# Turning all softmax tiles in place on VectorE, with stepped keys and four-term weights

## The chip, the cores and the metric

The kernel runs on one core of a Trainium2 chip, as a single launch. The metric is device time in microseconds (us); the time of a version is the median of its runs. A profiled execution gives the span from the first to the last instruction, which is a little shorter than the device time of the same execution.

## What is computed

A transformer block in float32 for 4 sequences (batches) of 512 tokens of width 512: a layer norm, and on its result both an attention with 16 heads and an MLP, added to the input. The MLP's weights are not stored but interpolated from control points by a cubic spline.

```python
xn = layernorm(x)                                     # x: (4, 512, 512)
q, k, v = (xn @ W + b for each of q, k, v)            # 16 heads of 32
scores = q k^T / sqrt(32) + slope[h] * arange(-511, 1)   # by key
attn = softmax(where(causal, scores, lowest))
ctx = attn v
a = ctx @ Wo + bo
gate_w, up_w = spline(gate_cp), spline(up_cp)         # (2048, 512)
down_w = spline(down_cp)                              # (512, 2048)
m = (silu(xn @ gate_w^T) * (xn @ up_w^T)) @ down_w^T
out = x + a + m
```

`spline` evaluates a Catmull-Rom cubic: every weight is a sum of four neighbouring control points times four coefficients that depend only on the weight's place.

## The kernel before

The kernel has two phases. The attention phase (to about 388 us of the span) holds the norms, the projections, the softmax and the making of most of the interpolated weights; the MLP phase follows, batch after batch.

**Units and groups.** Heads are taken four at a time: a group is one batch and four heads (`hg`), and there are 16 groups, g = 0 to 15, four to a batch. A unit is one group and one block `i` of 128 queries, so a group has four units; unit `i` has `i+1` blocks of 128 keys below the diagonal. A loop over `n`, one step per unit and three more at the end (`LAG`), writes out the order by hand; the helper `in_order` then keeps each engine's instructions in the order in which they were issued. In step `n`:

- `scores` multiplies queries by keys on TensorE into four PSUM banks, one per head (L865; a single set of banks, which the next unit reuses), and VectorE adds the distances and takes the extreme in one pass into the tile `p{i}` (L878), one buffer per `i`;
- `exponentials` runs on ScalarE (ACT; L894), in place;
- `normalize` takes the reciprocal of the sums on VectorE (L907) and multiplies on GpSimd (POOL; L909), for the unit of the step before;
- turning, so that keys lie across partitions for the product with the values. Two ways are mixed. Key blocks 0 and 2 are turned by TensorE, 128x128 at a time against the identity, into PSUM (L922, `turn`, three steps late), and copied by ACT to `pT` (L923). Key blocks 1 and 3 (`SLOTS`) are turned by VectorE in blocks of 32x32 into a tile of their own, `blocks` (L937, `swap`, two steps late), and four transfers on the SP queue, one for each strip of 32 partitions, put the blocks in place in `moved` (L945), which has one buffer;
- `values` (L966), once a group: 16 matmuls from `pT`, `moved` and `v` into one bank, called c here; ACT copies it out (L981). For group g they are issued in the last step of group g+1.

Since the two ways leave the keys of a block in different orders, ACT writes kT in halves (L816, L817), the second half stepped by four, and there are two distance tables, `dists`.

Around this, `items` and `small` put work into chosen steps: the projections of q and k for the next group (L798), of v (L837), the turning of the normed input (L767 on VectorE, L782, L783), the output projection of the batch before (L482, L489), the moments of the input that the MLP needs (`stretch_moments`, L510 to L525), input loads. POOL issues copies of laid-out rows to DRAM (L546). With a budget of microseconds a step, `some_weights` puts in VectorE's multiply and add steps of the weights: the row weights (gate and up, 8 terms, L646 and L649, coefficients times points that are broadcast to 32 partitions), and after them the down weights (5 and 4 terms, L690 and L693).

**The MLP phase** follows the strings in `plans`: G is a gate product of a quarter of the hidden width, U an up product (with its product on VectorE, L1157, a copy on POOL, L1158, and transfers), V an up product in the other set of banks, P an output projection of the last batch, F a load of features, X copies of rows, m, M, R, S, T moments and sums for the down product, L a load of the residual.

Of the kernel before, what the change touches and what calls it, by code (L numbers as in the profile page):

```python
# [18 lines left out]
P = 128  # L19
# [4 lines left out]
NB = D // P  # L24
# [6 lines left out]
SLOTS = [(1, 1), (2, 1), (3, 1), (3, 3)]  # L31
# [17 lines left out]
NCV = 5  # L49
NX = 9 + 4  # L50

COPIES = (1, 1, 4, 1)
NW, NW4 = 11, 4
NST = NW4 + 1

DOWN_STEPS = [("v", lo, hi, c) for lo, hi in ((0, 5), (5, 9)) for c in range(NCV)]
DOWN_STEPS += [("m", 0, NB, c) for c in range(4)]
# [277 lines left out]

def own_points(parts, points):


    values = parts[:, :, :, :9].transpose(0, 4, 3, 1, 2)
    values = values.reshape(P, 9, 2, P // 2, NCD)  # L340
    moments = parts[:, :, :, 9:].transpose(3, 4, 0, 1, 2)
    moments = moments.reshape(P, NB, 2, P // 2, NCD)
    strip = np.broadcast_to(points[:, None, None], (NB, Q32, 9, P, NCD)).reshape(values.shape)
    group = np.broadcast_to(points[None], (P, NB, P, NCD)).reshape(moments.shape)
    own = {}
    for kind, a, number, n in (("v", values, strip, NCV), ("m", moments, group, 4)):
        hit = (a != 0.0).any(axis=3)
        first = np.where(hit.any(axis=3), hit.argmax(axis=3), 0)
        first = np.minimum(first, NCD - n)[:, :, :, None, None] + np.arange(n)
        first = np.broadcast_to(first, (*a.shape[:4], n))  # L350
        few = np.take_along_axis(a, first, axis=4)
        assert np.count_nonzero(few) == np.count_nonzero(a)
        shape = (*a.shape[:2], P, n)
        own[kind] = few.reshape(shape), np.take_along_axis(number, first, axis=4).reshape(shape)
    steps = [[a[:, lo:hi, :, c].reshape(-1) for a in own[k]] for k, lo, hi, c in DOWN_STEPS]
    return *(np.concatenate(a) for a in zip(*steps)),
# [20 lines left out]
_coef = _coef.reshape(NB, NB, P, NCG, 2, Q32).transpose(3, 1, 5, 0, 4, 2)  # L377
COEF = single(_coef.reshape(NCG, P, NB, 2, P))
# [20 lines left out]
def block_kernel(  # L399
# [67 lines left out]
    dists = [wp.tile([P, S], F32, name=f"dist{k}") for k in range(2)]  # L467
# [35 lines left out]
    def stretch_moments(b):  # L503
# [15 lines left out]
        for k, ps in enumerate(banks):  # L519
            n = 64 if k == 2 else P  # L520
            o = xtp.tile([P, S], F32, name="out", bufs=2)
            if k == 1:
                nc.scalar.copy(o[:n], ps[:n])
            else:
                nc.vector.tensor_copy(o[:n], ps[:n])  # L525
            for s, (at, half) in place.items():
                if at == k:
                    nc.sync.dma_start(out=rows[s], in_=o[half * 64 : (half + 1) * 64])
# [23 lines left out]
    with ExitStack() as att:  # L552
# [36 lines left out]
        for k, dist in enumerate(dists):  # L589
            for t in range(NB):  # L590
                part = dist[:, t * P : (t + 1) * P]
                shape, steps = part, [[1, P]]
                if t % 2 == k:
                    shape = part.rearrange("p (r y) -> p r y", y=Q32)
                    steps = [[1, NB], [NB, Q32]]
                nc.gpsimd.iota(
                    shape,
                    pattern=steps,
                    base=1 - S + t * P,
                    channel_multiplier=0,  # L600
                    allow_small_or_imprecise_dtypes=True,
                )
                if t == NB - 1:
                    nc.gpsimd.affine_select(
                        out=shape,
                        in_=shape,
                        pattern=[[-step, n] for step, n in steps],
                        compare_op=ALU.is_ge,
                        fill=NEG,
                        base=0,  # L610
                        channel_multiplier=1,
                    )
# [3 lines left out]
        def row_weight_steps(first_down):  # L616
            size = NB * 2 * P
            shaped = lambda a: a.rearrange("p (q x n) -> p q x n", q=NB, x=2)
            spare = [
                feat[0].rearrange("p c h s -> p (c h s)")[:, k * size : (k + 1) * size]  # L620
                for k in range(4)
            ]
            temps = [wd[:, :size], wd[:, size : 2 * size]]
            tabs, points = {}, {}

            def load(c):
                def go():
                    tabs[c], points[c] = (shaped(a) for a in spare[c % 2 * 2 :][:2])
                    nc.sync.dma_start(out=tabs[c], in_=coef[c])
                    for k in range(NB):  # L630
                        strip = slice(k * Q32, (k + 1) * Q32)
                        nc.sync.dma_start(
                            out=spare[c % 2 * 2 + 1][strip],
                            in_=rowpts[c, k].partition_broadcast(Q32),
                        )
# [3 lines left out]
            def term(c, w):  # L639
                to = wT[:, :, 2 * w : 2 * w + 2, :]  # L640
                tmp = shaped(temps[w]) if c else to

                def times():
                    own = points[c].rearrange("p (w q) x n -> p w (q x) n", w=2)[:, w]
                    own = own.unsqueeze(2).to_broadcast([P, NB, 2, P])
                    nc.vector.tensor_tensor(tmp, tabs[c], own, ALU.mult)  # L646

                def plus():
                    nc.vector.tensor_tensor(to, to, tmp, ALU.add)  # L649

                return [times, plus] if c else [times]

            steps = [(0.0, load(0)), (0.0, load(1))]
            for c in range(NCG):
                for w in range(2):
                    steps += [(1.2, half) for half in term(c, w)]
                if c + 2 < NCG:
                    steps.append((0.0, load(c + 2)))
                elif c + 2 == NCG:
                    steps += first_down  # L660
            return steps


        def down_steps():
            size = 5 * P
            spare = feat[0].rearrange("p c h s -> p (c h s)")
            given, at = [], 0
            for _, lo, hi, _ in DOWN_STEPS:
                given.append((at, (hi - lo) * P))
                at += P * (hi - lo) * P  # L670

            def load(n):
                def go():
                    at, width = given[n]
                    for k, source in enumerate((downtab, downpts)):
                        to = spare[:, (n % 3 * 2 + k) * size :][:, :width]
                        part = source[at : at + P * width].rearrange("(p x) -> p x", p=P)
                        nc.sync.dma_start(out=to, in_=part)

                return go  # L680

            def term(n):
                kind, lo, hi, c = DOWN_STEPS[n]
# [679 lines left out]
```

## Time and profile before

| | |
|---|---|
| device time, median of 3 runs | 544.58 us (543.7 to 544.58) |
| device time of the profiled execution | 543.63 us |
| its span | 541.4 us |
| granted TensorE clock, mean | 0.993 |
| bytes moved by transfers | 92.98 MB |

The profile names a group of instructions by the line of the program, the engine, the operation and the tiles, output first (`p<-s,dist`). PE is TensorE's matmuls, PEld its loading of weights, DVE VectorE, ACT ScalarE, POOL GpSimd, SP the engine that issues most transfers; a trailing q is an engine's queue. Behind the bar of a group stand its busy time, the mean of one instruction, and the idle time just before the group with what ended it. A float32 matmul is recorded twice, a transpose once. The ends of matmuls are modelled, and neighbours on one engine overlap by some tenths of a microsecond, so a row's sum can be above what the engine was held.

### The profile page before, as it was taken

Reading aid. Unit: us, or ns where it says so; the run is one execution under the profiler, and the core shown is the slowest. Engines: PE = TensorE matmul, PEld = TensorE weight load, DVE = VectorE, ACT = ScalarE, POOL = GpSimd, SP = SyncE. Lnnn points to the kernel's source line nnn. Section 1 sums busy time; section 2 is a strip of 40 time slices with the busy share of each in tenths; the row PEclk is TensorE's granted clock in tenths of the full one; section 3 lists DMA queues with packets and bytes.
Section 4 is the critical chain, followed back from the end, with each engine's and each line's share of the span. In section 5 each row is a group of like instructions: output and inputs, shape, how many; then the busy total and the mean of one; then the engine's idle time right before and its main releaser. Section 6 shows DMA issues by size and latency. Waiting matters only on the chain.

```text
span 541.4 us, 12182 instructions
## 1 busy us (share of the span) xinstructions
PE 530.3 (98%) x4268; PEld 268.0 (50%) x4268; DVE 352.8 (65%) x990; ACT 296.0 (55%) x798; POOL 243.8 (45%) x436
## 2 busy tenths in 40 slices
PE   7999999999999999999999999989999999999997
PEld 6645545444445544444554454545334555747552
DVE  6169978888677877667676456563135584865836
ACT  2466875665466665646757588883313433624222
POOL 3045635574266565446656567671017232332310
PEclk9999999999999999999999999979999999999999
DMA  8933487575545785745743325464656565665344
GB/s 317 321 122 70 114 213 215 160 194 155 161 144 147 243 276 166 214 142 146 215 123 89 92 67 148 137 188 118 174 165 197 184 221 197 199 203 181 119 164 166
DMA packets 63805, 92.98 MB, mean 172 GB/s; under 512 B 10528, under 2 KB 35104, under 8 KB 63232
## 3 DMA queue, kind: packets, MB, share of 16 engines
q1 hardware_dynamic: 59136, 83.79, 51.5%
q0 software_dynamic: 4608, 8.40, 5.3%
q8 instruction: 34, 0.56, 0.4%
q14 instruction: 27, 0.22, 0.1%
HBM read 50.74 MB, written 23.68 MB: 137 GB/s over the span
## 4 chain that ended last, share of the span: by engine, by line
PE 84%; DVE 5%; DMA 5%; ACT 3%; SPq 2%; issue 1%; DVEq 0%; ACTq 0%
PE mm L798 17%; PE g L1135 9%; PE mm L837 9%; PE s L865 7%; PE mm L922 7%; PE mm L482 6%; PE o L1236 6%; PE c L966 5%; PE o L1182 4%; PE o L1253 3%; PE o L482 3%; ACT p L894 2%; DVE p L878 2%; PE s L482 2%; PE mm L510 2%; PE o L1135 2%
## 5 line engine op out<-in xcount | busy, mean ns | idle before, releaser
L909 POOL TENSOR_SCALAR p<-p,inv 128x128 f32<-128x128 f32 (+3 forms) x256 | 147.5, 589 | 172.1 <-DVE inv L907 122.1
L894 ACT ACTIVATE p<-p,low 128x128 f32<-128x128 f32 (+3 forms) x256 | 141.3, 555 | 48.9 <-DVE low L878 48.3
L878 DVE CUSTOM_DVE_ANT_0 p<-s,dist 128x128 f32<-128x128 f32 (+3 forms) x256 | 108.8, 481 | 21.8 <-PE s L865 21.5
L1158 POOL COPY made<-inner 128x512 f32<-128x512 f32 x64 | 38.9, 637 | 104.2 <-DVE inner L1157 81.5
L923 ACT COPY pT<-mm 128x512 f32<-128x512 f32 x96 | 54.8, 577 | 40.3 <-PE mm L922 40.0
L1135 PE MATMUL g<-feat,wT 32*64 32x512 f32 x864 | 65.3, 592 | 0.0
L1150 ACT ACTIVATE act<-g 128x512 f32<-128x512 f32 x64 | 33.0, 602 | 57.0 <-PE g L1135 56.7
L865 PE MATMUL s<-kT,qT 32*128 32x512 f32 (+3 forms) x512 | 57.4, 479 | 2.2 <-DVE low L878 2.0
L798 PE MATMUL mm<-xnT,wk 128*128 128x512 f32 (+1 forms) x136 | 59.3, 579 | 0.2 <-ACT xnT L783 0.2
L837 PE MATMUL mm<-wv,xnT 128*128 128x512 f32 x128 | 58.1, 596 | 1.1 <-ACT xnT L783 1.1
L798 PE MATMUL mm<-xnT,wq 128*128 128x512 f32 (+1 forms) x136 | 57.8, 567 | 0.0
L922 PE MATMUL mm<-ident,p 128*128 128x128 f32 x384 | 56.5, 283 | 0.4 <-ACT pT L923 0.3
L922 PEld LDWEIGHTS mm<-ident,p 128*128 128x128 f32 x384 | 42.5, 142 | 25.6 <-issue 17.1
L894 ACT ACTIVATION_READ_ACCUMULATOR p<-p,low 128x1 f32 x256 | 48.8, 191 | 0.0
L937 DVE STREAM_TRANSPOSE blocks<-p 128x512 f32<-128x512 f32 x64 | 43.4, 696 | 0.0
L1157 DVE TENSOR_TENSOR inner<-g,act 128x512 f32<-128x512 f32 x44 | 27.3, 683 | 21.7 <-PE g L1135 10.7
L1135 PEld LDWEIGHTS g<-feat,wT 32*64 32x64 f32 x864 | 30.6, 131 | 21.3 <-issue 10.6
L865 PEld LDWEIGHTS s<-kT,qT 32*128 32x128 f32 x512 | 24.5, 186 | 32.8 <-issue 16.2
L798 PEld LDWEIGHTS mm<-xnT,wk 128*128 128x128 f32 x136 | 24.5, 189 | 25.1 <-issue 21.5
L546 POOL DMA_DIRECT2D table<-samples x64 | 36.9, 583 | 0.0
L1236 PE MATMUL o<-inner,dRM 32*64 32x512 f32 x512 | 36.6, 588 | 0.0
L798 PEld LDWEIGHTS mm<-xnT,wq 128*128 128x128 f32 x136 | 24.7, 190 | 22.4 <-issue 21.7
(105 smaller groups left out, 656.3 us busy)
## 6 DMA issues: line engine op xcount, KB each, us to landing
moved<-blocks SPq DMA_DIRECT2D x128, 64.0 KB, 2.1
moved<-blocks SPq DMA_DIRECT2D x64, 128.0 KB, 3.0
feat<-table SPq DMA_DIRECT2D x16, 512.0 KB, 4.3
inner<-made SPq DMA_DIRECT2D x32, 256.0 KB, 3.5
table<-samples POOLq DMA_DIRECT2D x64, 88.0 KB, 3.0
xp<-in_xp_dram SPq DMA_DIRECT2D x16, 256.0 KB, 5.1
feat<-in_coef_dram SPq DMA_DIRECT2D x8, 512.0 KB, 8.8
feat<-in_rowpts_dram SPq DMA_DIRECT2D x32, 128.0 KB, 5.1
```

The source lines that it names most:

```text
L482: nc.tensor.matmul(ps, lhsT=wsb["o"][:, c, r * P : (r + 1) * P], rhs=ctxT[b][:, c, :], start=(c == 0), stop=(c == NB - 1),)
L798: nc.tensor.matmul(ps[0][:, tokens], lhsT=wsb[name][:, c, hg * P : (hg + 1) * P], rhs=xnT[b][:, c, tokens], start=(c == 0), stop=(c == NB ...
L837: nc.tensor.matmul(ps[0], lhsT=xnT[b][:, c, t * P : (t + 1) * P], rhs=wsb["v"][:, c, :], start=(c == 0), stop=(c == NB - 1),)
L865: nc.tensor.matmul(banks[b, hg][j][:, at : at + (k + 1) * P], lhsT=qk[b, hg, "q"][rows, k * P : (k + 1) * P], rhs=qk[b, hg, "k"][rows, : ( ...
L878: nc.vector.tensor_tensor_reduce(out=p[:, j, :nk], in0=ps[j], in1=dists[i % 2][:, S - nk :], scale=-SLOPES[hg * NG + j], scalar=BIG, op0=A ...
L894: nc.scalar.activation(p[:, j, :nk], p[:, j, :nk], AF.Exp, bias=low[:, j : j + 1], scale=-1.0, accum_out=total[:, j : j + 1],)
L909: nc.gpsimd.tensor_scalar(p[:, j, :nk], p[:, j, :nk], inv[:, j : j + 1], 1.0, ALU.mult, ALU.mult)
L922: nc.tensor.transpose(ps[:, j, :], p[:, j, c * P : (c + 1) * P], ident)
L923: nc.scalar.copy(pT[b, hg, c][:, :, (i - c) * P : (i - c + 1) * P], ps)
L937: nc.vector.transpose(own[:, :, k].rearrange("p r j k -> p j r k"), soft[u][0][:, :, c * P : (c + 1) * P].rearrange("p j (r k) -> p j r k" ...
L1135: nc.tensor.matmul(ps[k][cols, :], lhsT=wT[rows, q, 2 * w + part, cols], rhs=feat[b][rows, q, part, :], start=(part == 0), stop=(part == 1),)
L1236: nc.tensor.matmul(sums[b][r][cols, :], lhsT=dR[rows, a, cols], rhs=o[rows, :], start=(a == 0), stop=False,)
```

## The change

- **Turning.** `turn`, `pT` and their ACT copies are gone. `p` is laid out as (strip r, key block c, head, 32), `swap` turns the whole tile in place with one VectorE instruction per unit (512, 1024, 1536 or 2048 elements a partition), and four transfers per unit move it to `moved`, now with 13 slots, one buffer. Row block 0's move is held until after the value matmuls of the group before have been issued.
- **Keys.** All keys of a block are in one stepped order: ACT writes kT with one instruction, TensorE reads it by a view, and there is one distance table.
- **Order.** In a step, the scores now come ahead of the normalizing of the unit before.
- **Weights.** Row weights have 4 terms, each with a point for every coefficient (loaded, not broadcast); down weights have 4 terms throughout and are made in the MLP phase, under the new letter D in the first plan, with two buffers.
- **Engines.** Value copies and moment copies go from VectorE to ACT, the norms of batches 1 to 3 from VectorE to POOL.

```diff
-SLOTS = [(1, 1), (2, 1), (3, 1), (3, 3)]
+NSLOT = 3 * NB + 1
+TERMS = (0.6, 0.2, 0.8, 0.2)
-DOWN_STEPS = [("v", lo, hi, c) for lo, hi in ((0, 5), (5, 9)) for c in range(NCV)]
-DOWN_STEPS += [("m", 0, NB, c) for c in range(4)]
+DOWN_STEPS = [("v", lo, hi, c) for lo, hi in ((0, 5), (5, 9)) for c in range(TAPS)]
+DOWN_STEPS += [("m", 0, NB, c) for c in range(TAPS)]
...
+    dist = wp.tile([P, NB, NB, Q32], F32, name="dist")
...
-                nc.vector.tensor_scalar(
+                (nc.gpsimd if b else nc.vector).tensor_scalar(
...
-                    nc.vector.tensor_copy(vals[b][:, t, :], ps[0])
+                    nc.scalar.copy(vals[b][:, t, :], ps[0])
...
+                keys = qk[b, hg, "k"].rearrange("p (c r y) -> p r c y", r=NB, y=Q32)
...
-                            rhs=qk[b, hg, "k"][rows, : (k + 1) * P],
+                            rhs=keys[rows, :, : k + 1],
...
-            p = sp.tile([P, NG, nk], F32, name=f"p{i}")
+            p = sp.tile([P, NB, i + 1, NG, Q32], F32, name=f"p{i}")
...
-            ps = ps_m.tile([P, NG, P], F32, name="mm")
-            for j in range(NG):
-                nc.tensor.transpose(ps[:, j, :], p[:, j, c * P : (c + 1) * P], ident)
-            nc.scalar.copy(pT[b, hg, c][:, :, (i - c) * P : (i - c + 1) * P], ps)
...
+            if i == 0:
+                moved[b, hg] = tp.tile([P, NB, NSLOT, NG, Q32], F32, name="moved")
+            own = soft.pop(u)[0]
+            flat = own.rearrange("p r c j k -> p (r c j k)")
+            nc.vector.transpose(flat, flat)
             to = moved[b, hg]
             def move():
                 for a in range(NB):
                     nc.sync.dma_start(
-                        out=to[:, a, at].rearrange("p s j k -> p (s j k)"),
-                        in_=own[a * Q32 : (a + 1) * Q32].rearrange("p r s j k -> p r (s j k)"),
+                        out=to[:, a, 3 * i : 4 * i + 1].rearrange("p c j k -> p (c j k)"),
+                        in_=own[a * Q32 : (a + 1) * Q32].rearrange("p r c j k -> p r (c j k)"),
                     )
...
+            for move in held:
+                move()
+            held = []
             if 0 <= n - LAG_SWAP < len(units):
                 move = swap(units[n - LAG_SWAP])
+                if (n - LAG_SWAP) % NB:
+                    move()
+                else:
+                    held.append(move)
+            credit = min(credit + TERMS[n % NB] - 0.25 * len(small[n]), 1.0) if n >= NB else 0.0
+            late = []
+            while done < len(row_terms) and credit > 0.0:
+                row_terms[done]()
+                done += 1
+                credit -= 1.0
...
+    def down_terms():
+        size = 5 * P
+        spare = [
+            midp.tile([P, NB, S], F32, name="res").rearrange("p c s -> p (c s)"),
+            xpp.tile([P, NB, D], F32, name="xp").rearrange("p c s -> p (c s)"),
+        ]
...
+            yield
+            nc.vector.tensor_tensor(tmp, part(n, 0), part(n, 1), ALU.mult)
+            if n + 2 < len(DOWN_STEPS):
+                load(n + 2)
+            if c:
+                yield
+                nc.vector.tensor_tensor(to, to, tmp, ALU.add)
...
-        "G0 P0 U0 F0 P1 G1 P2 U1 F1 X4 P3 G2 V2 F2 X4 G3 V3 F3",
+        "G0 P0 D2 U0 D1 F0 P1 D2 G1 D1 P2 D2 U1 D1 F1 X4 P3 D2 G2 D2 V2 D1 F2 X4 D2 G3 D2 V3 D3 F3",
```

## The prediction

> **What bounds the kernel now.** I read the page's busy shares first, then its costliest groups, then stretches of time, and last TensorE's and the SP queue's timelines.
>
> ```profile
> PE 530.3 (98%) x4268; PEld 268.0 (50%) x4268; DVE 352.8 (65%) x990; ACT 296.0 (55%) x798; POOL 243.8 (45%) x436
> L922 PE MATMUL mm<-ident,p 128*128 128x128 f32 x384 | 56.5, 283 | 0.4 <-ACT pT L923 0.3
> L923 ACT COPY pT<-mm 128x512 f32<-128x512 f32 x96 | 54.8, 577 | 40.3 <-PE mm L922 40.0
> L937 DVE STREAM_TRANSPOSE blocks<-p 128x512 f32<-128x512 f32 x64 | 43.4, 696 | 0.0
> ```
>
> TensorE is busy nearly always, and L922, the turning of softmax tiles, is its own work. The stretches (columns: length; busy time of PE, PEld, DVE, ACT, POOL; granted clock; DMA share; GB/s) show where that holds:
>
> ```profile
> 158.60:182.60 24.00, 24.00 (x137) 12.21 (x136) 17.59 (x49) 17.46 (x50) 14.26 (x23) 1.00 0.53 151
> 319.90:333.40 13.50, 13.26 (x100) 7.04 (x99) 8.89 (x37) 11.61 (x37) 10.80 (x22) 1.00 0.55 149
> 352.00:370.00 18.00, 15.74 (x84) 8.36 (x82) 10.45 (x41) 12.67 (x40) 10.44 (x20) 0.81 0.59 166
> 387.80:417.60 29.80, 29.80 (x299) 12.14 (x303) 11.07 (x18) 10.23 (x18) 10.11 (x18) 1.00 0.59 181
> ```
>
> The first is a head group of batch 1: TensorE full, VectorE at 73%. The second, of the last batch, has no projections for a next batch and is short. The last is the MLP's first stage, where VectorE has room.
>
> ```profile
> 177.84 0.40 PE L966 MATMUL c<-moved,v 128*32 128x128 f32 x8
> 178.17 0.66 PE L922 MATMUL mm<-ident,p 128*128 128x128 f32 x4
> 178.66 0.60 PE L782 MATMUL mm<-ident,xn 128*128 128x128 f32 x4
> 160.50 0.71 DVE L937 STREAM_TRANSPOSE blocks<-p 128x512 f32<-128x512 f32 x1
> 165.72 1.29 DVE L937 STREAM_TRANSPOSE blocks<-p 128x512 f32<-128x512 f32 x2
> 79.20 2.49 SPq L945 DMA_DIRECT2D moved<-blocks  x4
> moved<-blocks SPq DMA_DIRECT2D x128, 64.0 KB, 2.1
> moved<-blocks SPq DMA_DIRECT2D x64, 128.0 KB, 3.0
> inner<-made SPq DMA_DIRECT2D x32, 256.0 KB, 3.5
> ```
>
> Durations of neighbours overlap. Eight transposes hold TensorE 0.87 us in the chain of waits, so 0.109 each and not 283 ns. Two VectorE transposes take 1.29, so 0.59 each. Four moves cost the SP queue 2.49 us to issue, 0.62 each, before the last one's landing time begins.
>
> **TensorE's side.** 384 transposes x 0.109 = 41.8 us go, 24 or 2.6 us in each of 16 head groups. Stepped keys are only another reading order: the value matmuls already read `moved` in runs of 32 (128x384: 487 ns, the contiguous 128x384 scores 541), so nothing. ACT loses 54.8 us of copies and takes over value copies (16 x 0.58) and moment copies (8 x 0.59), still below. ACT's stepped write of kT costs 466 ns against 471, so stepped exponentials cost nothing; for POOL's stepped normalizing no row exists: 4 x 0.675 us (2.70 for four of 512 elements) to 4 x 1.92 (its longest); I take the first, the commonest. POOL's 12 norms (0.6 to 0.9 each) fall into its idle 172 us.
>
> **VectorE's side.** A 1024-wide tensor op takes 1264 ns, a 512-wide one 739, so 1.03 ns an element; transposes of 512, 1024, 1536, 2048 are then 0.70, 1.23, 1.76, 2.29, together 5.98 a group, 95.7 in all: +52.3. (Bounds for 2048: 2.1, slope alone, to 2.8, four of 512.) Row weights: 30 ops, 37.5 us, become 14, 17.5: -20.0. Down weights (19.1), value copies (11.1), moment copies (5.5) and 12 norms (7.2, to POOL) leave: -42.9. Net -10.6, so VectorE's sum is no bound.
>
> The skill's page "VectorE: DVE Perf Modes", section "Rules for kernel authors", advises TensorE for a 128x128 transpose if PSUM will do, and so speaks against the change. Its table gives 311 ns per 128x128 (bf16) on VectorE; 384 more would be an estimated 119 us instead of the trace's 52, some 4 us more in every group, and VectorE would then stand level with TensorE. The trace's 0.59 per 512 elements decides.
>
> **The wait that is added.** The tile p is now turned in place and read by the transfers, so the next group's scores of the same row block wait until its four moves landed. `moved` has one buffer too: row block 0 of group g is moved only after the value matmuls c of group g-1. Together they form a loop from one c to the next, counted from c's end (us):
> - move of block 0: four issues, last at 1.9, landing 2.1, and 0.1 to be seen: 4.1;
> - scores reduction of block 0 (four starts 0.21 apart in VectorE's timeline): 4.95; reciprocal and transpose of block 2: 6.7;
> - block 1's move is queued behind block 0's on SP, landing at 2.5+4.6 = 7.1 (1.9 + 3.0, less 0.3 as the median already holds queueing); its reduction, four of 0.35: 8.5;
> - reciprocal and transpose of block 3: 10.9;
> - move of block 3, four of 256 KB: 1.9 + 3.4, the inner<-made row: 16.2 (bounds: 4.0 by out_dram<-res at 2.1, 7.0 by xp<-in_xp_dram at 5.1);
> - c itself, 2.3: 18.5.
>
> SP issues 256 moves instead of 192 (+40 us of issuing) and 24 row-point loads fewer (0.46 each, -11); that counts only where it lies in the loop above. Behind the waiting reductions stand all reciprocals and transposes of VectorE; TensorE waits for them through the single set of score banks, and through c. A weight op (1.25) in the first step adds 0.8, in groups 4, 8, 12 and 13. With 0.5 for other transfers (the moves carry 41.9 MB for 16.8, and the DMA share goes from about 0.55 to 0.7 or 0.75) the floor is 19.0, or 19.8.
>
> **The sum over groups.** c ends in TensorE's timeline at 57.3, 78.2, 100.8, 123.6, 158.1, 178.2, 201.5, 223.8, 253.4, 273.5, 296.1, 316.0, 332.8, 349.4, 368.9, 387.9. Each stretch less 2.6, or the floor if that is more: 19.0 (was 20.9), 20.0 (22.6), 20.2 (22.8), 31.9 (34.5), 19.0 (20.1), 20.6 (23.2), 19.8 (22.3), 27.0 (29.6), 19.0 (20.1), 20.0 (22.6), 19.8 (19.9), 19.8 (16.9), 19.0 (16.6), 19.0 (19.5): 294.1 for 311.6, -17.5. The last: block 3 is turned about 7 after c, moved, and c follows; with the queue behind three mid stores, 16.6 for 18.9: -2.3. The first c, behind two steps full of VectorE work: +0.8. Where loop and TensorE are within a microsecond (about eight stretches) the later one wins each time: +3. Attention: -16.
>
> In the last batch TensorE will stand idle for several us a group; one such place was granted 0.81 of the clock for 18 us, 3.4 us of clock. Where the loop binds, most of that is waiting anyway: +2 (0 to 6).
>
> The skill's page "TensorE: Matmul & The Clock Gate" (Part 1) has the clock fall to half after an idle window of about 3.4 us and rise after as much work; by it each of the last three groups would lose some 1.7 us, an estimated 5 in all.
>
> **The MLP's first stage.** 12 down-weight steps with 6.8 MB of loads enter 29.8 us that already move 5.4 MB. VectorE's 21 ops (15.7 us) beside 11.1 fit. But two buffers let a load start only when the step two before has multiplied: two DMAs, 0.5 + about 4 us, plus the op, 5 us for two steps. The first loads queue behind the xt loads that landed 6.9 us into the stage: step 0 multiplies at about 8.5, steps 2 to 10 five times 5 later, and once V2's products (2.7) stand between: 36. V3's products are queued behind it on VectorE and hold the PSUM banks that the next batch's first moments (31 us into the stage) need: +6, between 3 (loads at the 3.3 of in_downtab_dram) and 9 (at xp's 5.1).
>
> Sum: -16 + 2 + 6 = -8. The profiled execution took 543.63 (span 541.4, 2.2 around it), the median of the three is 544.58; 535.6 by the one, 536.6 by the other: 536.5.
>
> **Rivals.**
> 1. *The floor lies below TensorE* (.16). If block 3's move takes 4.0 and nothing contends, the floor is near 17: the 14 stretches sum to 282, -29; with -2.3, +0.8, +1 for fewer ties, +2 and 3 in the MLP that is -25: 520. For it: four 64 KB moves are through in about 4. Against: blocks 1 to 3 have 2 to 4 times that.
> 2. *The loop is longer* (.28). Eight stretches sit on the floor and three are within 1.2 us, so the first microsecond more costs 8 and the second 11; from a floor of 20.0 (20.8) on, the change loses. At 21, about what block 3's move at 7.0 gives, the stretches sum to 313, +2; with -2.3, +0.8, +1, +2 and +6 that is +9: 554. For it: landing times of moves reach 7.4 and the coefficient loads take 8.8 on the same queue. Against: the medians.
> 3. *The MLP stalls* (.06): with loads at the 8.8 of in_coef_dram the six pairs take 53 us and hold V3 back 22 instead of 6: 552.
> 4. *No change* (.06): the removed 41.8 given back almost exactly. That transposes of p stay on TensorE is ruled out: the built program has only those of x.
>
> Forecast case .44, 527 to 543. The three runs differ by 0.16%, so 0.2% is what can be told. Faster .44 + .16 = .60, same .06, slower .28 + .06 = .34. Range 522 to 553, leaving a tenth on either side; the forecast's own range is 527 to 543.
>
> **What would show it.** TensorE's L922 group is gone and its busy share falls; waits of VectorE's reduction on DMA `moved` appear (none now); c stands 19 to 20 us apart also in the last batch, longer than now; the MLP's first stage has a TensorE wait of some us before the moments; transposes 2048 wide take 2.2 to 2.3. Wrong if c follows TensorE's sums alone, or if VectorE is the bound outside those waits.

## The result, and the profile after

The changed kernel took 623.62 us (median of 4, 622.11 to 626.14) beside 544.41 us for the kernel before (4 runs on the same chip): ratio 1.146, 95% interval 1.142 to 1.151. Its profiled execution has a span of 620.9 us (541.4 before), with a granted clock of 0.906 (0.993). The forecast of 536.5 and its range of 522 to 553 were wrong, in sign too.

The page's busy shares and the granted clock by slice:

```profile
PE 528.2 (85%) x3884; PEld 256.1 (41%) x3884; DVE 367.1 (59%) x934; ACT 260.7 (42%) x710; POOL 266.7 (43%) x440
PEclk9997988789998988997989868669897889999999
```

384 matmul records are gone, and yet TensorE's busy time is about the same 528 us: the matmuls last longer. The clock record alternates between full and half speed, with some 116 us of the span at half (6.8 before). The chain of work that ended last has moved from TensorE to transfers and the queue that issues them. Here are its shares by engine before, then by engine and by line after:

```profile
PE 84%; DVE 5%; DMA 5%; ACT 3%; SPq 2%; issue 1%; DVEq 0%; ACTq 0%
```

```profile
PE 48%; DMA 18%; SPq 10%; DVE 9%; issue 8%; POOL 6%; ACT 2%; DVEq 0%; POOLq 0%; ACTq 0%
DMA moved<-p 10%; SPq L855 7%; PE mm L731 6%; PE g L1030 6%; PE mm L767 6%; PE c L870 6%; PE o L1131 5%; PE mm L484 4%; POOL p L839 4%; PE o L1077 4%; DVE p L810 4%; PE s L797 4%; DVE p L850 3%; PE o L1148 2%; POOL xn L700 2%
```

The waits (total us, times, longest) show the new order. L810 is VectorE's reduction, L870 the value matmuls c, L715 the transposes of x:

```profile
DVE p L810 <- DMA moved<-p: 78.8, 35, 6.3
PE s L797 <- DVE low L810: 26.4, 9, 7.0
PEld mm L715 <- POOL xn L700: 19.5, 8, 3.6
PE mm L715 <- POOL xn L700: 13.9, 6, 2.8
PE c L870 <- DMA moved<-p: 11.7, 4, 3.8
```

VectorE stands in front of a tile p that is still being read by its transfers; behind it TensorE waits for the score banks. The first two lines are one mechanism, not two costs to add.

By stage: c ends first at 63.5 us (57.3 before), last at 443.8 (387.9). So the attention is 55.9 us longer and what follows, 177.1 for 153.5, 23.6 longer. Of the 15 stretches from one c to the next, before's were 16.6 to 34.5; now nine are between 23.5 and 25.1, the shortest is 22.7, and the four of the last batch are 24.2, 23.8, 24.7 and 23.5 (16.9, 16.6, 19.5 and 18.95 before).

One of these four, 371.84 to 395.63, follows the prediction's loop step by step in VectorE's timeline (start, duration, idle time before and what ended it; c had ended at 371.84):

```profile
376.07 0.29 DVE L810 CUSTOM_DVE_ANT_1 p<-s,dist 128x128 f32<-128x128 f32 x1 [4.54 <-DMA moved<-p]
377.01 1.75 DVE L850 STREAM_TRANSPOSE p<-p 128x1536 f32<-128x1536 f32 x1
379.75 0.42 DVE L810 CUSTOM_DVE_ANT_1 p<-s,dist 128x256 f32<-128x256 f32 x1 [0.99 <-DMA moved<-p]
381.22 2.28 DVE L850 STREAM_TRANSPOSE p<-p 128x2048 f32<-128x2048 f32 x1
391.27 0.69 DVE L810 CUSTOM_DVE_ANT_0 p<-s,dist 128x512 f32<-128x512 f32 x1 [3.49 <-DMA moved<-p]
```

and TensorE's:

```profile
385.71 3.50 PE L797 MATMUL s<-kT,qT 32*128 32x512 f32 x8 [3.47 <-DVE low L810]
391.51 4.12 PE L870 MATMUL c<-moved,v 128*32 128x512 f32 x32 [2.30 <-issue]
```

Block 0's move is over 4.2 us after c, block 1's 7.9, block 3's transpose 11.7, block 3's move 19.4 (7.8 for that move alone), and c itself lasts 4.1 us instead of 2.36. The stretch has TensorE busy 17.5 of 23.8 us at 0.78 of the clock; the kernel before, busy without a pause in 158.60 to 182.60, was granted 1.00 there:

```profile
371.80:395.60 23.80, 17.47 (x88) 8.09 (x84) 12.88 (x40) 11.08 (x35) 12.32 (x24) 0.78 0.64 160
443.80:497.00 53.20, 39.19 (x320) 18.07 (x320) 23.35 (x36) 11.35 (x19) 12.79 (x20) 0.88 0.77 251
```

The second line is the MLP's first stage up to the first moments, 53 us where before needed 31. The first moments before (c had ended at 387.87) and after (443.79):

```profile
418.88 0.61 PE L1182 MATMUL o<-inner,basist 32*64 32x512 f32 x4
```

```profile
497.06 6.00 PE L1077 MATMUL o<-inner,basist 32*64 32x512 f32 x60 [7.54 <-issue]
```

### The profile page after: what moved, and what is told of

Same layout as the page of the kernel before. It is cut to its first block, busy times and chain, and to the rows that moved or that the text cites. A ratio compares the mean times of both kernels' runs of the same rounds, so it can differ in the third digit from the quotient of the medians.

```text
span 620.9 us, 11506 instructions
## 1 busy us (share of the span) xinstructions
PE 528.2 (85%) x3884; PEld 256.1 (41%) x3884; DVE 367.1 (59%) x934; ACT 260.7 (42%) x710; POOL 266.7 (43%) x440
## 4 chain that ended last, share of the span: by engine, by line
PE 48%; DMA 18%; SPq 10%; DVE 9%; issue 8%; POOL 6%; ACT 2%; DVEq 0%; POOLq 0%; ACTq 0%
DMA moved<-p 10%; SPq L855 7%; PE mm L731 6%; PE g L1030 6%; PE mm L767 6%; PE c L870 6%; PE o L1131 5%; PE mm L484 4%; POOL p L839 4%; PE o L1077 4%; DVE p L810 4%; PE s L797 4%; DVE p L850 3%; PE o L1148 2%; POOL xn L700 2%
## 5 line engine op out<-in xcount | busy, mean ns | idle before, releaser
L839 POOL TENSOR_SCALAR p<-p,inv 128x128 f32<-128x128 f32 (+3 forms) x256 | 145.0, 578 | 202.3 <-DVE inv L837 201.4
L825 ACT ACTIVATE p<-p,low 128x128 f32<-128x128 f32 (+3 forms) x256 | 140.6, 550 | 126.8 <-DVE low L810 123.8
L810 DVE CUSTOM_DVE_ANT_1 p<-s,dist 128x128 f32<-128x128 f32 (+2 forms) x192 | 69.8, 420 | 95.6 <-DMA moved<-p 47.4
L850 DVE STREAM_TRANSPOSE p<-p 128x512 f32<-128x512 f32 (+1 forms) x64 | 94.8, 1482 | 0.1
L797 PE MATMUL s<-kT,qT 32*128 32x512 f32 (+3 forms) x512 | 67.3, 515 | 26.4 <-DVE low L810 26.4
L870 PE MATMUL c<-moved,v 128*32 128x128 f32 (+3 forms) x512 | 55.0, 587 | 31.4 <-DMA moved<-p 11.7
L1030 PE MATMUL g<-feat,wT 32*64 32x512 f32 x864 | 72.1, 611 | 4.1 <-DVE inner L1052 4.1
L810 DVE CUSTOM_DVE_ANT_0 p<-s,dist 128x512 f32<-128x512 f32 x64 | 40.4, 687 | 49.1 <-DMA moved<-p 31.4
L797 PEld LDWEIGHTS s<-kT,qT 32*128 32x128 f32 x512 | 31.3, 197 | 59.7 <-issue 29.2
L870 PEld LDWEIGHTS c<-moved,v 128*32 128x32 f32 x512 | 20.6, 138 | 77.5 <-issue 67.1
L1030 PEld LDWEIGHTS g<-feat,wT 32*64 32x64 f32 x864 | 37.1, 136 | 23.7 <-DVE inner L1052 7.4
L767 PEld LDWEIGHTS mm<-wv,xnT 128*128 128x128 f32 x128 | 25.4, 210 | 31.8 <-issue 27.6
L731 PEld LDWEIGHTS mm<-xnT,wk 128*128 128x128 f32 x136 | 25.3, 190 | 28.1 <-issue 27.3
```

Source lines behind the costliest of these rows:

```text
L731: nc.tensor.matmul(ps[0][:, tokens], lhsT=wsb[name][:, c, hg * P : (hg + 1) * P], rhs=xnT[b][:, c, tokens], start=(c == 0), stop=(c == NB ...
L767: nc.tensor.matmul(ps[0], lhsT=xnT[b][:, c, t * P : (t + 1) * P], rhs=wsb["v"][:, c, :], start=(c == 0), stop=(c == NB - 1),)
L797: nc.tensor.matmul(banks[b, hg][j][:, at : at + (k + 1) * P], lhsT=qk[b, hg, "q"][rows, k * P : (k + 1) * P], rhs=keys[rows, :, : k + 1], ...
L810: nc.vector.tensor_tensor_reduce(out=p[:, :, :, j], in0=ps[j].rearrange("p (r c y) -> p r c y", r=NB, y=Q32), in1=dist[:, :, NB - 1 - i :] ...
L825: nc.scalar.activation(by_head(p)[:, :, j], by_head(p)[:, :, j], AF.Exp, bias=low[:, j : j + 1], scale=-1.0, accum_out=total[:, j : j + 1],)
L839: nc.gpsimd.tensor_scalar(by_head(p)[:, :, j], by_head(p)[:, :, j], inv[:, j : j + 1], 1.0, ALU.mult, ALU.mult)
```

## The experiments

Each was timed beside the kernel before on the same chip; times are medians, mostly of two runs 2 to 7 us apart. "Less" is against the changed kernel's 623.62, which was not run again beside them. The theory: the loop from one c to the next, through the single buffers of `moved` and p, sets the attention's pace, and its longest piece is the transfers of block 3. Rivals: normalizations on POOL, SP's issuing, TensorE's half clock, and for the MLP the operations rather than the loads.

**1. Normalizations back on VectorE.**

```
-                (nc.gpsimd if b else nc.vector).tensor_scalar(
+                nc.vector.tensor_scalar(
```

> The changed kernel with one part undone: the 12 normalizations of x for batches 1 to 3 are on VectorE again (546 ns each before) and not on POOL (2062 each). Theory (the loop through p and moved sets the time in nearly every head group): the six groups with normalizations in which TensorE waited for xn (13.9 + 19.5 us of its waits, the two kinds partly the same places) get some of that back, the other ten nothing: 8 to 15 us less, 609 to 616. Rival (the normalizations on POOL are the main cause of the +79.5): 30 us or more less, under 594. No part at all: 622 to 625.

618.02 us, 5.6 less. The rows of L700 in the changed kernel and in this one (duration minimum, median and maximum in ns):

```profile
L700 POOL TENSOR_SCALAR xn<-xp,mean,rstd x12: 2062/2062/2085, 64.0 to 290.4; 128x512 f32<-128x512 f32 x12
```

```profile
L700 DVE TENSOR_SCALAR xn<-xp,mean,rstd x16: 496/544/939, 5.6 to 286.0; 128x512 f32<-128x512 f32 x16
```

A real cost, but less than the 8 to 15 that were expected and far below the rival: the last batch, which has no such step, keeps stretches of 24.0 to 26.4.

**2. The moves from two queues.**

```
-                    nc.sync.dma_start(
+                    (nc.scalar if a % 2 else nc.sync).dma_start(
```

> The changed kernel with every second of the four transfers of a move issued from ACT's queue and not from SP's. Theory (the 7.8 us of block 3's move are 2.5 us of issuing, with the fourth issue held back, and then the last landing of 4.7): with two issues a queue the last is issued at 0.6, the move takes about 5.5 and block 0's 2.9 instead of 4.2, so the loop gets 2 to 3 us shorter and 10 to 13 groups follow: 25 to 35 us less, 590 to 600. Rival (the transfers' data is what lasts, the DMA engines or their order at the other end): landing of the last stays at 7 to 8 us after the first issue and the time within 5 us of 623.6. ACT's waiting at its issues may cost exponentials: then ACT's waits on DVE L850 or on DMA show, and the time is longer.

620.63 us (618.25 and 623.02): the rival. The issues do come sooner, but the landings get longer, here the changed kernel's and then this one's (KB each, median us from issue to landing):

```profile
moved<-p SPq DMA_DIRECT2D x64, 256.0 KB, 4.7
```

```profile
moved<-p SPq DMA_DIRECT2D x32, 256.0 KB, 6.1
moved<-p ACTq DMA_DIRECT2D x32, 256.0 KB, 6.6
```

In the groups where no other move comes between, block 3's four transfers take 6.9 to 7.7 us from the first issue to the last packet in the changed kernel and 6.7 to 8.4 here. So who issues them matters little; what was saved in issuing went into the landing.

**3. The down-weight loads only once.**

```
-            if n + 2 < len(DOWN_STEPS):
-                load(n + 2)
```

> The changed kernel with only the first two pairs of loads of the down-weight steps in the MLP's first stage; the steps multiply the same two pairs again, so the down weights are not the reference's. All 21 VectorE operations stay. Theory (VectorE's products stand behind multiplications that wait for loads that SP issues late): first moments 31 to 35 us into the stage instead of 53, 18 to 22 us less, 602 to 606. Rival (the operations themselves, or the cold TensorE clock, make the stage longer): first moments at 48 or later, at most 6 us less.

603.94 us, 19.7 less. The first moments come 34.3 us into the stage (479.44 less c's end at 445.18) instead of 53.3:

```profile
479.44 1.19 PE L1077 MATMUL o<-inner,basist 32*64 32x512 f32 x6 [0.56 <-issue]
```

All VectorE operations are still there, so they (and the clock) cost at most the 3 us that are left over the kernel before's 31; the loads and the waits for them are the other 19. In the changed kernel SP reaches several loads only after the stores of `inner` and `lone`, for which it waits itself, and VectorE's products stand behind the multiplication that needs the load:

```profile
495.67 0.69 DVE L1184 TENSOR_TENSOR res<-res 128x512 f32<-128x512 f32 x1 [6.65 <-DMA res<-in_downpts_dram]
496.28 2.47 DVE L1052 TENSOR_TENSOR inner<-o,act 128x512 f32<-128x512 f32 x4
```

**4. `moved` by row block, with one and with two buffers, and p with two.** All three split `moved`; the control has one buffer of everything. The second version has two for each part of `moved` and issues block 0's move at once; the third, whose line for p stands last here, has two for each p. (Both make the down-weight and edge tiles after the attention, for room.)

```
-                moved[b, hg] = tp.tile([P, NB, NSLOT, NG, Q32], F32, name="moved")
+            to = tp.tile([P, NB, i + 1, NG, Q32], F32, name=f"moved{i}", bufs=1)
...
+            for i in range(NB):
+                w = moved.pop((b, hg, i))
+                for c in range(i + 1):
...
-            p = sp.tile([P, NB, i + 1, NG, Q32], F32, name=f"p{i}")
+            p = sp.tile([P, NB, i + 1, NG, Q32], F32, name=f"p{i}", bufs=2)
```

> The changed kernel with the loop's first link cut: the moved tile is four tiles by row block, each with two buffers, so block 0's move is issued right after its transpose and no longer waits for the value matmuls; these are 40 of 128 columns instead of 16 of 128 to 512. (Room comes from the down-weight tile and two edge tiles, made after the attention.) p keeps its single buffers. Theory (the loop from one c to the next sets the stretches): what is left is p3's own round, reduction 2.8, what VectorE does until its transpose about 5, transpose 2.3, move 7.8, near 18; stretches fall from 24 to 18 to 20 in the last batch and to TensorE's sums (20 to 22) elsewhere, attention ends 30 to 50 us sooner, 575 to 595. Rival (TensorE's half clock or the transfers' total volume set the pace, not the order of waits): stretches stay at 23 to 25, 615 to 630.

> The control of the run with two buffers: moved as four tiles by row block, but with one buffer each, and the value matmuls by row block, 40 of 128 columns. Theory (order of waits): the move of block 0 needs only the first four value matmuls, so it starts some 1.5 us before c's end, and only block 3's 16 matmuls wait for block 3's move: 1 to 2 us less in each group, 595 to 612; the second buffers then brought the rest of the 17.7. Rival (the transfers' volume sets the pace): 618 to 626.

> Moved as four tiles with one buffer each, as in the control, and the softmax tiles p with two buffers each (room again by making the down-weight and edge tiles after the attention). VectorE's reductions then wait for no transfer; what is left of the loop is c, the moves of the four blocks one after the other (16 issues; block 3's last), c. Theory (the waits of VectorE's reductions for moves, 78.8 us in the changed kernel, are the loop's costly part): these waits vanish, stretches 18 to 21 in the last batch, 570 to 590. Rival (the moves themselves, 2.6 MB a group, take as long as the stretch): stretches 22 to 24 and the wait moves to c, 600 to 620.

Control 612.68, `moved` with two buffers 605.88, p with two buffers 595.34. The control alone gives 10.9, or 0.7 a group, just short of the 1 to 2 that were expected: block 0's move is issued before c ends in 11 of 15 groups (0.8 to 5.4 us before), where in the changed kernel it followed c in all. The two buffers of `moved` add only 7 more, since p's own round stays (VectorE still waits 68.1 us for moves there); this missed its expected 575 to 595. Those of p give 17.3, a little less than the 570 to 590 that was expected asks for. With them no reduction waits for a move any more, and the wait has gone to c, as that run's waits show:

```profile
PE c L863 <- DMA moved<-p: 31.8, 12, 7.5
PEld c L863 <- DMA moved<-p: 11.4, 4, 7.8
```

So the theory's mechanism is there, but it was not all, and the rival was right about where the wait would go: the attention still ended at 415.3. Something behind the buffers holds c.

**5. Half of block 3's bytes.** On the control:

```
+            kept = min(i + 1, 2) if i == NB - 1 else i + 1
...
-                            rhs=w[:, :, c, j],
+                            rhs=w[:, :, c % 2 if i == NB - 1 else c, j],
```

> The control with four moved tiles, but of block 3's softmax only the first two key chunks are moved (128 KB in each of four transfers instead of 256), and the value matmuls use these twice: half of block 3's value product is left out of the computation and the number of instructions and packets is the same. Theory (block 3's move is as long as its data): 7.8 becomes 4 to 5, 2.5 to 4 us less in each stretch that the loop sets, 30 to 50 us below the control. Rival (the fixed part, issuing and the number of packets, is what lasts): at most 10 us below the control.

593.09, 19.6 below the control: between the two expectations. Block 3's move itself became as short as the theory said: where its four issues follow one another its last packet is through 4.2 to 4.6 us after the first issue, for the changed kernel's 6.9 to 7.2. But VectorE's reductions still wait 45.8 us for moves here (81.9 in the control), so a next wait is near. The clean test is on a version in which p no longer waits.

**6. The parts together, and then half of block 3's bytes.**

> The changed kernel with the parts that helped alone put together: moved by row block and two buffers for each p (595.3 alone), the 12 normalizations on VectorE (5.6 less alone), and the loads of the down-weight steps issued from ACT's queue, with all data, instead of from SP's behind the stores (19.7 less when they were left out). Theory (three separate causes): the sum, 566 to 575. Rival (they cover one another, or the loads' own time is what VectorE waits for): 580 to 592. Either way it is not below the kernel before, since the moves of 2.6 MB a group stay.

> The put-together version of the changed kernel (577.64: moved by row block, two buffers for each p, normalizations on VectorE, down-weight loads from ACT's queue), with only the first two of four key chunks of block 3 moved and used twice, so that half of block 3's value product is left out: 2.1 MB of moves a group instead of 2.6. Theory (with the buffers of p out of the way, what stays is the length of the moves between two c): block 3's move 2.5 to 3 us shorter in the groups where c waits for it, 25 to 40 us less, 540 to 553. Rival (order, not bytes: the moves start only after c because moved has one buffer): 8 us less at most, 570 to 577.

Together 577.64, between the two expectations; with 2.1 instead of 2.6 MB of moves a group 546.70, 30.9 less or 1.9 us for each group, as expected. That lands on the kernel before (ratio 1.003, interval 1.000 to 1.006), with half of block 3's value product missing. The attention then ends at 373.9, 14.0 before the kernel before's 387.9, while the MLP part stays 20 longer. A stretch in which hardly anything waits shows what the removed transposes are worth: the first group of the first batch after c, 57.28 to 78.18 before and 59.14 to 77.02 here:

```profile
57.28:78.18 20.90, 20.77 (x127) 10.80 (x126) 18.25 (x58) 16.56 (x49) 11.32 (x19) 1.00 0.70 167
```

```profile
59.14:77.02 17.88, 17.39 (x150) 9.23 (x150) 15.51 (x49) 12.91 (x40) 8.89 (x16) 1.00 0.51 113
```

3.0 us shorter, at full clock. The number of packets is the same in both versions (72,065 in the span). The bytes of the moves between two c's are therefore the largest single cost found.

In the put-together version the down-weight loads went to ACT's queue. That gave 9.3 us at most of the 19.7 (the part after the attention took 172.1 for 181.4): the wait moved. On ACT each activation now follows, in the order of the program, issues that themselves wait (the one ahead of the first line here stands at 421.65):

```profile
422.30 2.06 ACT L1046 ACTIVATE act<-g 128x512 f32<-128x512 f32 x4 [13.10 <-DMA inner<-made]
434.43 2.06 ACT L1046 ACTIVATE act<-g 128x512 f32<-128x512 f32 x4 [10.07 <-DMA inner<-made]
```

**7. Keeping TensorE's clock up.** Six, then three matmuls whose result nobody reads:

```
+            keep_warm(6)
             ps = ps_c.tile([P, S], F32, name="c")
```

> The changed kernel with six more 128x512 matmuls (0.46 us each, 2.8 us) on TensorE right before the value matmuls of every head group; nothing reads their result. They fill the idle time in which TensorE waits for block 3's move. Theory (the half clock after such waits costs time itself: c 3.7 to 4.5 us long instead of 2.36 in 10 of 16 groups, and c lies in the loop): c stays near 2.4, 1.5 to 2 us less in each of these ten, 15 to 25 us less, 600 to 608. Rival (the clock only stretches work beside which TensorE waits anyway, or the added matmuls are late themselves): 620 to 635, with the share of half clock smaller all the same.

> The earlier run with added matmuls was sized wrongly: a 128x512 matmul is two records of 0.46 us, so six of them held TensorE 5.5 to 7 us and not 2.8. Here three of them (2.8 us) stand only in the last batch and before block 3's scores, where TensorE waits 3.5 us for the reduction of block 2. Theory (half clock in the loop costs): block 3's scores fall from 3.50 to 2.06 and c from 4.1 to 2.4 in these four groups, 2.5 to 3 us less each, 10 to 13 in all. Rival (the half clock lies beside waits that last anyway): within 3 us of the changed kernel, with c short.

671.88 and 626.03: both missed. In the first the extra work was mis-sized: two records each, 5.3 to 8.0 us a group instead of 2.8. It does price the half clock in one way. In the stretch ending at 437.27, the same group as the one shown above, stand

```profile
427.64 7.33 PE L865 MATMUL mm<-wv,ident 128*128 128x512 f32 x12
434.91 2.36 PE L876 MATMUL c<-moved,v 128*32 128x512 f32 x32
```

The extra work took 7.33, filled 2.3 of waiting and made c 1.76 shorter (2.36 for 4.12); that sums to +3.3, and the stretch was 27.0 for 23.8, +3.2. Had c's length not counted, it would be +5.0. In the second the scores got shorter (2.55 for 3.50) but c was cold again (4.35 after a wait of 2.74), so its condition was not met. Some 1.8 us in each of ten groups with a long c is thus an estimate from one stretch and not shown; it would be a consequence of the waits.

**8. A smaller dose, on the kernel before.** Four key tiles of ten go VectorE's way in the kernel before. Here it is five, and then, in a second version, six (all of key chunks 1 to 3). The first version's edit begins:

```
-SLOTS = [(1, 1), (2, 1), (3, 1), (3, 3)]
+SLOTS = [(0, 0), (1, 1), (2, 1), (3, 1), (3, 3)]
```

> The kernel before with one tile of the change: key chunk 0 of row block 0 is no longer transposed by TensorE (4 transposes of 24 in a head group) but turned by VectorE into the blocks tile and moved, four transfers of 64 KB more a group (16.8 MB of moves become 21.0); its value product becomes 4 matmuls of 128 columns of its own. Separate blocks stay, so p waits for no transfer. Theory (transposes are worth 0.109 each as long as the moves and the waits behind them stay inside TensorE's time): 0.3 to 0.4 less a group where TensorE is the bound, 4 to 6 us in all, 538.5 to 541. Rival (any tile on the slow way costs more than TensorE's 0.44, by SP issuing, VectorE's 0.7 or transfers): 546 to 553.

> The kernel before with the tiles of key chunk 2 turned by VectorE and moved too, so that only chunk 0 is left to TensorE: 16 transposes a group instead of 24, moves of 25.2 MB instead of 16.8 (41.9 in the changed kernel), separate blocks as before, moved as one tile a row block, value matmuls of 128 columns for chunks 1 to 3. Row and down weights as before. Theory (the change loses because a group's moves are as long as its stretch and hold p and moved; at 1.5 MB a group they take some 10 us and no tile p waits): TensorE's 0.87 a group come out, 8 to 14 us less, 531 to 537. Rival (the price rises in step with the moved bytes from the first one on; half of the change's +56 us of attention goes with a third of the added 25.1 MB): 550 to 565.

554.75 (ratio 1.018, 1.013 to 1.023) and 553.56 (1.015, 1.009 to 1.021): both slower by 1.5 to 1.8%, outside the noise, where a gain was expected; the second lies in its rival's range, the first just above its own. With chunk 2 moved, six stretches are 0.7 to 1.6 shorter, around TensorE's 0.87; others lose more. For the one tile a shared buffer was suspected:

> The one-tile version of the kernel before, with one thing mended: block 0's turned tile has a buffer of its own and no longer shares that of block 2, whose transposes waited 16.6 us in 8 places for block 0's held move (554.75 then). Bytes moved are the same 21.0 MB. Theory (single buffers behind a move that waits for the value matmuls are what costs): these waits vanish and TensorE's 0.3 to 0.4 a group come out, 540 to 544. Rival (the bytes and SP's four issues cost): 550 to 556 again.

557.37: not the buffer. By its stretches 11.2 us of its loss lie in two groups (29.0 for 22.6, and 28.1 for 23.25), the ones in which the x loads and the 1 MB store of samples stand on SP's queue ahead of the moves. TensorE stops within c there:

```profile
99.76 0.83 PE L972 MATMUL c<-pT,v 128*32 128x384 f32 x8
105.29 1.46 PE L972 MATMUL c<-moved,v 128*32 128x384 f32 x8 [4.70 <-DMA moved<-blocks]
```

The last four took the x loads of batches 2 and 3, and likewise the stores of samples, off that queue:

```
-                nc.sync.dma_start(out=xpt[b][:, t], in_=xpf[r : r + P, :])
+                (nc.scalar if b > 1 else nc.sync).dma_start(out=xpt[b][:, t], in_=xpf[r : r + P, :])
```

> Control: the kernel before itself with those loads and stores on ACT's queue. TensorE is busy all the time in the groups concerned and waits for no move, so the same time, 544 to 547, by either theory; over 548 would mean that ACT's issuing costs exponentials.

> The one-tile version with its own buffer (557.37), with the x loads of batches 2 and 3 and the stores of the samples issued from ACT's queue instead of SP's. Its stretches were longer than before's by 6.4 us in group 2 and 4.8 in group 6, where these loads stand ahead of the moves, and within 0.5 elsewhere but for 1 to 1.3 in two. Theory (the place on the queue): 9 to 11 of the 12 us come back, 545 to 548, 2 to 3 below that only if ACT pays nothing. Rival (the DMA engines are full there, whoever issues): within 4 us of 557.

> The version with key chunk 2 on VectorE too (553.56; 16 TensorE transposes a group), with the same loads and stores on ACT's queue. Its stretches were 0.7 to 1.6 shorter than before's in five groups, 1.8 and 2.1 longer in groups 6 and 7, 3.8 longer in group 12, 3 in the first. Theory (the queue): groups 6 and 7 come back, 548 to 551. Rival: unchanged, 552 to 555.

> The put-together version of the changed kernel with all data (577.64), with the same loads and stores on ACT's queue. Its c waited 5 us for moves in each of groups 2 and 6. Theory (the queue): 4 to 9 us less, 568 to 574. Rival (the engines are full): 575 to 580. Either way above the kernel before.

The control itself went to 560.75 (1.027, 1.021 to 1.032), outside its expected 544 to 547, as its ACT stood behind its own issues (`ACT pT` waited 9.8 us at once for the samples' store). The one-tile version took 561.87 and the six-tile one 567.46, where the queue theory asked for 545 to 551, so this edit cannot tell queue from bytes for those two groups. Against this control the one tile costs 1.1 us (12.1 before) and its two groups are 2.2 and 2.4 longer (6.4 and 4.8 before), which fits the queue but does not show it; the six tiles still cost 6.7 (8.0 before). The put-together version took 575.36, within what two runs can tell from 577.64. No version with complete computation beat the kernel before.

## Why the prediction was wrong, point by point

- **TensorE's transposes, 2.6 a group.** Right, and a little low: 3.0 in a stretch where hardly anything waits. The prediction's own lines (178.17 to 178.66 for four) give 0.12 each and 2.9 a group. In the version with half of block 3's value product missing the attention ended 14.0 sooner, beside the forecast's 16; the changed kernel never gets there.
- **VectorE's sums, stepped access.** Right for the parts: transposes took 0.68, 1.22, 1.75 and 2.28 for the forecast 0.70, 1.23, 1.76 and 2.29, and stepped exponentials and normalizations were no dearer in sum (140.6 us for 141.3, and 145.0 for 147.5). The net of -10.6 did not show: VectorE is busy 261.9 us of the attention for 262.0 before. As forecast, its sum is no bound. The trace's row decided rightly against the higher figure of the Trainium skill's page "VectorE: DVE Perf Modes"; its advice, TensorE for a 128x128 transpose, held here for another reason, the moves that follow.
- **POOL's normalizations, "0.6 to 0.9 each" into idle time.** Wrong: 2.06 each, and on TensorE's way to the transposes of x. Undoing it gave 5.6 us.
- **The loop: this is the step that failed.** Its order was right to the step (4.1 forecast and 4.2 found, 7.1 and 7.9, 10.9 and 11.7), its last two terms were mis-sized. Block 3's move was put at 5.3 with a bound of 7.0, its landing from the row of another 256 KB transfer (the row says 3.5, the sum has 3.4). It took 7.8: with four of them under way each landed in 4.7, and the fourth was issued 2.6 us after the first and not 1.9. c was put at 2.3 and took up to 4.5, where TensorE had waited and the granted clock had fallen. 18.5 became 23.8. The floor was then above every group of the last batch and most others. By rival 2's own arithmetic (21 gives 554, and each further microsecond more than 11) 24 is about 590 from the loop: the mechanism was named, its size was cut off at 21. The range even ended at 553, below that rival's own 554, to which .28 had been given.
- **The ends of the attention.** The first c was put 0.8 later and came 6.2 later, since TensorE already waits in the steps of group 1: 2.77 us before its last scores, which took 3.50 for 2.24, and 2.27 before c, which took 4.50 for 2.35. The last stretch was put at 16.6 and took 23.5.
- **Clock, "+2 (0 to 6)".** Too small in kind: the prediction counted only the last batch's idle time and held that waiting covered it. The rows show 116 us at half clock, and c in the loop itself; what this cost in time is only estimated (experiment 7). The Trainium skill's page "TensorE: Matmul & The Clock Gate", Part 1, with its idle window of about 3.4 us, fits the record: the half-clock intervals last 3.4, 6.8, 10.2 or 17.1 us. Its estimated 5 us in the last batch fits the rows better than 2: three of the four c's there took 1.4 to 1.8 longer than 2.36, 4.8 in all. Both leave out that the other batches would wait too.
- **The MLP's first stage, +6.** The forecast's range of +3 to +9 failed on the loads: 19 us for them (shown by leaving them out), at most 3 for the operations. The forecast queued the loads behind one another, not behind stores that SP itself waits for. Rival 3's 22 came, but by luck, since its condition, loads that land in 8.8, did not. Of the rows of these loads two have a median, 5.8 for the tile `xp` and this:

```profile
res<-in_downpts_dram SPq DMA_DIRECT2D x2, 320.0 KB, 5.0
```

- **Sum.** Attention +55.9 for -16 + 2, MLP +23.6 for +6. Of the attention's 70 us above the forecast, 62.7 lie in the fourteen stretches (356.8 for 294.1), 5.4 in the first c and 6.9 in the last stretch, less the 5 that had been set apart for ties and clock. Parts are not additive to the last microsecond; measured one on another they are 10.9 (block-wise release of `moved`), 17.3 (p held by its transfers), 17.7 (normalizations, and loads on another queue) and 30.9 (0.5 MB of moves a group). What stays open is how much of the loss in the two groups of experiment 8 in which loads and stores share the queue is its order and how much the bytes. Of the change's other parts, the order within a step, the row weights of four terms and the copies given to ACT were not undone alone.

## What to carry to other kernels

Before taking work from a full engine, add up the bytes that the other way moves between two uses of the same buffer, at the rate at which several such transfers land together, and set that against the stretch; the median of other transfers of the same size was too low here (3.5 for 4.7). A tile that is transformed in place and then read by transfers is held for the length of those transfers, and a loop through it has to be given its upper end as a case of its own, with the clock at which a waiting TensorE will run (0.78 in the stretch shown). A queue change is no free repair: in the control of experiment 8 ACT's copies waited 9.8 us behind an issue of its own.

## What was not expected of the hardware

- POOL's tensor_scalar with two per-partition scalars on 128x512 took 2062 ns, VectorE's 544, while POOL's normalization with one such scalar took about 0.68.
- Four 256 KB transfers issued from two queues instead of one landed in 6.1 and 6.6 us each instead of 4.7; the four together were no sooner through.
- In the changed kernel the value matmuls, issued after waits, took 3.7 to 4.5 us instead of 2.36 in ten of sixteen groups.
- The x loads of batches 2 and 3 and the stores of samples, issued from ACT instead of SP, made the kernel before 14 us slower.
